# A four-layer graph network on one core: the order of work around layers 1 and 2, with two chunks' slab sums stored later

## The chip, the cores and the metric

The kernel runs on 1 core of one Trainium2 chip. The metric is the device time of one execution in microseconds (us). Engines are named as in the profile: PE (TensorE matmul), PEld (TensorE weight load), DVE (VectorE), ACT (ScalarE), POOL (GpSimd), SP (SyncE, which here issues most DMAs).

## What is computed

A stack of four layers on 3327 nodes with 256 features each, every layer in the form x = x + layer(relu(layernorm(x)), adj). The adjacency matrix is 3327 x 3327, sparse in its values but stored dense.

```
x = x + adj @ (h @ W0.T + b0)                                     # layer 0
sim = tanh(adj * adj) * (adj > 0); keep the 700 largest of a row   # layer 1
x = x + relu(sim @ (tanh(h @ Wp + bp) @ Wg) + bg)
A = adj + I; d = A.sum(1) ** -0.5                                  # layer 2
x = x + relu((d[:, None] * A * d[None, :]) @ (h @ W2.T))
# layer 3: two steps of propagation with (adj + I), rows scaled to sum 1,
# and of top-p attention over all nodes; projections; a last layer norm
```

Layers 0 to 2 are each a product of the whole adjacency matrix with node rows; layer 3 has such products too, and attention.

## The kernel before

**Tiles and products.** The nodes are 26 blocks of 128, taken as two halves of 13; a *pair* p is block p with block p + 13. Each layer multiplies 2 x 2 quadrants of slabs (128 x 128 tiles of the transposed adjacency matrix, loaded by SP) with seven products in place of eight. For that DVE makes four sums of slabs for each chunk (`Feed.adding`, L607 to L610: s1, a difference written over quadrant 21, s2, s4) and four sums of nodes for each stretch of node rows (`combining_nodes`, L396 to L399, into the tile `ts`). In layer 2 the identity is added to diagonal slabs first (L606).

**Layer 0** goes pair by pair, in three chunks of node blocks (`CUTS`). A pair's seven products gather in one `ps_row` tile of two banks; `result` adds them up on DVE (L683 to L688), `finish0` makes the new rows of x (L931 to L937), and the next layer's nodes follow: layer norm (L416, L417, the root on POOL at L125, L433), transposes on PE (`turn`, L445), and a projection (`hidden`, L457, then L504 on DVE and L505 on ACT).

**Layers 1 and 2** go by *doubles* of two pairs (pair 12 alone at the end), in five chunks of 3, 3, 3, 2, 2 node blocks (three chunks for pair 12). `Double.steps` (L744) runs in each chunk through the products in the order 1, 2, 5, 4, 6, 3, 7, one matmul for a node block; a step is one such matmul (two records in the profile), so that in a chunk of three blocks steps 0 to 2 are product 1, 3 to 5 product 2, 6 to 8 product 5, 9 to 11 product 4, 12 to 14 product 6. Products 1, 2, 4, 5 gather in the first of two accumulator tiles, 6, 3, 7 in the second. Both have the tag "row" of the pool `ps_row`, which holds two buffers: a double takes both, and so does its successor. `Double.result` reads the first tile with two ACT copies (L777), and the second with DVE (L779, L781, L782, the last of which completes y1). `weighed` (L789) then multiplies y0 and y1 with the layer's weights, and `finish1` or `finish2` makes the new rows of x.

**What sets the order.** PE's order is written by hand: a layer is a sequence of steps, and `hooks` say after which step of the next double (or pair) an older one's stage is put (its weighing, its turn, its keys). DVE, ACT, POOL and SP are put in order by a scheduler from priorities and due times. `Feed.upto(n)` issues, ahead of chunk n, the loads as far as chunk n + 2 and the sums as far as chunk n + 1, and stores of sums. Slab tiles have three buffers, so a chunk's loads wait until PE has released the chunk three before it.

**Kept sums.** Layer 3 needs the same slab sums as layer 0. They are kept in `s_dram`: those in `KEPT_FIRST` are stored by SP (L637) during layer 0, the others (`KEPT_LATER`) in layer 2; for stored sums of layer 0 POOL adds the identity in layer 3 (L1401).

**Around the change.** At the start of layer 1 (`doubles`, L800 on), pair 11's and pair 12's turn and projection of layer 0's results still come as hooks (30, 40) of the first double; node sums of blocks 9 to 11 are combined ahead of everything and those of block 12 in the last chunk. At the end of layer 2 what remains of the last stages runs after the last product: keys (`add_nodes`, L290: four times a projection into one bank of `ps_acc`, read by ACT at L298 and L302) and the weighing of pair 12. Layer 3 begins with four DVE sums over all node rows (`combining`, L1379 to L1382), the sum of the keys (L1172), their mean on PE (L1168), their centring on DVE (L1179, L1182), and the logits (L1202), among products with slabs (L1462).

Of the kernel before, what the change touches and what calls it, by code (L numbers as in the profile page):

```python
# [11 lines left out]
F32 = mybir.dt.float32  # L12
# [5 lines left out]
ALU = mybir.AluOpType  # L18
AX = mybir.AxisListType
# [5 lines left out]
P = 128  # L25
# [5 lines left out]
H = T // 2  # L31
CUTS = ((0, 5), (5, 9), (9, 13))
# [2 lines left out]
    (p, k)  # L35
    for p in range(2, H)
    for c, (a, b) in enumerate(CUTS)
    if (p + c) % 3
    for k in range(a, b)
}  # L40
PIECE = 6
# [15 lines left out]
def kernel(  # L57
# [22 lines left out]
    nc = tc.nc  # L80
# [86 lines left out]
    def merged(*plans):  # L167
        out = {}
        for p in plans:
            for k, v in p.items():  # L170
                out.setdefault(k, []).extend(v)
        return out
# [109 lines left out]
    def add_nodes(kT, ksum, xT, m, name, bank):  # L282


        n = P
        acc = bank(f"pkq_{name}")
        r, col = (0, m) if m < LOW else (DA, m - LOW)
        i = 0 if m < LOW else 1
        for c in range(NC):
            nc.tensor.matmul(  # L290
                acc[:, :n], kq[:, c, i : i + 2].rearrange("p i e -> p (i e)"), xT[:, c, :n],
                start=(c == 0), stop=(c == NC - 1),
            )
        q = DA - r
        real_n = min(n, N - m * P)
        at = slice(m * P, m * P + n)
        with tc.high_priority():
            nc.scalar.activation(  # L298
                kT[r : r + DA, col * P : col * P + real_n], acc[r : r + DA, :real_n], AF.Copy,
                accum_out=ksum[r : r + DA, m : m + 1],  # L300
            )
            last_key.append(nc.scalar.copy(qT[q : q + DA, at], acc[q : q + DA, :n]))  # L302
        nc.scalar.dma_start(qT[r : r + DA, at], qT[q : q + DA, at])
# [9 lines left out]
    def layers_0_to_2(again):  # L313
# [11 lines left out]
        tag = "b" if again else "a"  # L325
# [75 lines left out]
        def combine_nodes(rhs, a, b):  # L401
            run(combining_nodes(rhs, a, b))
# [60 lines left out]
        class Pair:  # L463
# [60 lines left out]
                with tc.high_priority():  # L524
                    nc.scalar.copy(self.rhs.pair(self.p), acc)

            def keys(self):
                for i in range(2):
                    m = self.p + i * H
                    add_nodes(kT0, ksum0, self.xT[:, :, i * P : (i + 1) * P], m, f"{self.name}_{i}", self.bank)  # L530


        def scaled_nodes(p, rhs, x2):
# [20 lines left out]
        class Feed:  # L554
# [67 lines left out]
            def upto(self, n):  # L622


                self.store(n - 1)
                for k, (ahead, what) in enumerate(((2, self.load), (1, self.add))):
                    while self.done[k] < min(n + ahead + 1, len(self.order)):
                        what(*self.order[self.done[k]])
                        self.done[k] += 1
                    if not k:  # L630
                        self.store(n)
# [58 lines left out]

        WHERE = {2: (48, 64), 4: (20, 34, 50, 64)}

        def products(rhs, feed, finish, pair_after, following, counted, begin):

# [98 lines left out]
        def doubles(layer, rhs, feed, w, finish, todo, at_first, places, pair_after, following=None, counted=None):  # L795

            if not todo:
                for c in CUTS:
                    combine_nodes(rhs, *c)
            n = 0  # L800
            for p in range(0, H, 2):
                prod = Double(layer, p, rhs, feed, w)
                first = not p and todo
                if first:
                    combine_nodes(rhs, CUTS[2][0], H - 1)
                hooks = dict(zip(places[prod.many - 1] if p else at_first, todo))
                if counted:
                    hooks[88] = functools.partial(counted, p, prod.many)
                for c, (a, b) in enumerate(cuts(prod.many)):
                    feed.upto(n)  # L810
                    for k, l in ((a, b - 1), (b - 1, b)) if first and b == H else ((a, b),):
                        if first and l == H:
                            combine_nodes(rhs, k, l)
                        for at in prod.steps(c, k, l):
                            if at in hooks:
                                hooks[at]()
                    n += 1
                    if prod.many == 1 and c and following:
                        combine_nodes(following, *CUTS[c - 1])
                feed.upto(n)  # L820
                left = todo[len(places[prod.many - 1]) :] if p else []
                prod.result()
                pairs = []

                def out(p, t, prod, pairs):
                    acc = prod.weighed(t)
                    with tc.high_priority() if p == H - 1 else nullcontext():
                        x2 = feed.x2.pop(p + t)
                        finish(p + t, x2, acc)
                        pairs.append(pair_after(p + t, x2))  # L830

                todo = [functools.partial(out, p, t, prod, pairs) for t in range(prod.many)]
                if layer == 2:
                    for stage in (Pair.turn, Pair.keys):
                        for t in range(prod.many):
                            todo.append(functools.partial(lambda what, pairs, t: what(pairs[t]), stage, pairs, t))
            if layer == 1:
                return todo
            for what in (*left, todo[0]):
                what()  # L840
            return pairs[0]

        def of_double(p):
# [66 lines left out]
        if not again:  # L910
# [138 lines left out]
            def second_layer(p, x2):  # L1049
# [3 lines left out]

            left = doubles(
                1, rhs1, Feed(1, OF_DOUBLES, from_rows(x1_dram), change=filtered, many=of_double), late_weights["wg"],
                finish1, left, (30, 40), ((20, 32), (10, 16)), second_layer, following=rhs2,
            )
        else:
            def x1_pair(p):
# [54 lines left out]
        left = doubles(  # L1114
            2, rhs2,
            Feed(2, OF_DOUBLES, from_rows(x2_dram), count=count2, keep=() if again else KEPT_LATER, many=of_double), w2s,
            finish2, left, (10,), ((20, 32, 56, 72), (10, 16, 38, 44, 52, 60)), lambda p, x2: Pair(3, p, h3, x2),
            counted=done2,
        )
        return lctx, h3.rows, kT0, ksum0, left  # L1120
# [16 lines left out]
    def layer_3_in(again, tag, big, ep, w3, sm3, h3, kT0, ksum0, left):  # L1137
# [20 lines left out]
        def constants():  # L1158
            for i in range(2):
                nc.scalar.dma_start(u1s[:, :, i, :], u1t[i].rearrange("(c p) e -> p c e", p=P))  # L1160
                nc.scalar.dma_start(u2s[:, :, i, :], u2t[i].rearrange("(c p) e -> p c e", p=P))

        def key_sum(kT, ksum, name):
            total = sm3.tile([P, 1], F32, tag="ktotal", name=f"ktotal_{name}{tag}")

            def by_tensor():
                pk = one_bank(f"pk_mean_{name}{tag}")
                nc.tensor.matmul(pk[:, :1], halves, total, start=True, stop=True)  # L1168
                return pk

            with tc.high_priority():
                nc.vector.tensor_reduce(total, ksum, AX.X, ALU.add)  # L1172
            return by_tensor

        def centre(kT, pk, name):
# [664 lines left out]
        with tc.manual_schedule(engines=PE_ALONE):  # L1840
# [3 lines left out]
            def prepare(step, m, kT):  # L1844
                made[m] = scores(step, m, kT)
                return made[m][2]
# [37 lines left out]
            def propagate_first(n, at):  # L1884

                d, phase = divmod(n, 4)
                x = firsts.setdefault(d, FirstPropagation(d)) if d not in firsts else firsts[d]
                units = len(x.units(phase))
                run(x.steps(phase), {int(k * units // T): v for k, v in at.items()})
                if n != T - 3 and n != T - 1:  # L1890
                    x.keep(phase)

            def whole_run(steps, at):

                return {at: [lambda: next(steps)]}
# [29 lines left out]
            for i in range(EARLY):  # L1925
                if i == 0:
                    left.pool, left.bank = (w3, "eT", 3), one_bank
                    mean0 = []

                    def sum_keys():  # L1930
                        mean0.append(key_sum(kT0, ksum0, "0"))

                    def centre_keys():
                        centre(kT0, mean0[0](), "0")

                    propagate_first(0, dict(zip((15, 18, 19, 22), ([what] for what in (*left.stages, sum_keys, centre_keys)))))
                    with tc.issue_after(last_key[-1].ins):
                        constants()
                    next(sums_of_first)
                elif i == 1:  # L1940
                    propagate_first(1, merged(whole_run(prepare(0, 0, kT0), 3), {12: [lambda: next(sums_of_first)]}))
                    run(find(0, 0, st0))
                    with tc.issue_after(added[-1].ins):
                        kT1, ksum1 = new_keys(f"1{tag}", big)
                else:
                    propagate_first(i, whole_run(prepare(0, i - 1, kT0), 3))
                    finder = find(0, i - 1, st0)
                    if i + 1 < EARLY:
                        run(finder)
# [250 lines left out]
```

## Time and profile before

| | |
|---|---|
| runs | 2493.24, 2492.91, 2490.91 us; median 2492.91 |
| profiled execution | 2493.01 us, of which the span of the profile is 2491.2 us |
| PE busy | 2449.1 us (98%) |
| DVE, ACT, POOL busy | 2079.9, 1074.7, 293.6 us |
| layer 1 begins, layer 2 begins, its products end | 332.7, 632.3, 928.4 us |
| SP's DMA packets | 367.5 MB on its main queue, 156 GB/s in all |

The profile lists groups of instructions by line, engine and operation; `out<-in` are tile names, `x` the count, then busy time, mean of one in ns, and the engine's idle time just before the group with what ended most of it. A row of the timeline is start, length, engine, line, operation, tiles, count, and in brackets the idle time before it and what released it. Times within the span are us from its start. Two records of L755 are one step of a double.

### The profile page before, as it was taken

The page shows a single profiled execution, that of the slowest core. Times are in us where ns is not written, and L with a number is a line of the kernel's source. Part 1 is how long each engine was busy: PE and PEld are TensorE (multiplying, and loading weights), DVE is VectorE, ACT ScalarE, POOL GpSimd, SP SyncE. Part 2 cuts the span into 40 slices and gives each one's busy share as a digit, 9 for nine tenths or more (in the row PEclk, how much of TensorE's full clock was granted, in tenths as well). Part 3 has the DMA queues.
Part 4 walks back from the last instruction along what each step waited for, and adds up shares of the span by engine and source line. Part 5 has one row for each costly group of instructions (what it writes and reads, how often), then busy time and mean ns, then how long its engine had stood idle before and what let it go on. Part 6 is the DMA issues. An engine that isn't in the chain of part 4 may idle for free. (4 is left out here: it accounts for less than half of the span.)

```text
span 2491.2 us, 41120 instructions
## 1 busy us (share of the span) xinstructions
PE 2449.1 (98%) x14483; PEld 2104.5 (84%) x14483; DVE 2079.9 (83%) x5306; ACT 1074.7 (43%) x2074; POOL 293.6 (12%) x466
## 2 busy tenths in 40 slices
PE   9999989999999999999999999999999999999997
PEld 8999978888888897777777777777788888888887
DVE  7877788888876758888788797885899999999994
ACT  3000034343011115556556665654556555655551
POOL 2000010000000000000000100000112322222232
PEclk9999999999999999999999999999999999999999
DMA  6788856565968656423232324324534443444343
GB/s 203 250 274 265 281 178 188 165 186 161 314 216 266 213 157 215 124 66 101 87 107 84 104 67 122 97 72 122 178 94 130 143 122 114 135 140 125 114 140 109
DMA packets 278675, 387.79 MB, mean 156 GB/s; under 512 B 24253, under 2 KB 216250, under 8 KB 278458
## 3 DMA queue, kind: packets, MB, share of 16 engines
q1 hardware_dynamic: 257322, 367.54, 47.7%
q10 hardware_dynamic: 21136, 17.52, 2.1%
q8 instruction: 116, 1.90, 0.3%
q14 instruction: 101, 0.83, 0.1%
HBM read 315.37 MB, written 67.89 MB: 154 GB/s over the span
## 5 line engine op out<-in xcount | busy, mean ns | idle before, releaser
L226 ACT COPY eT_a<-pt_a 128x512 f32<-128x512 f32 (+1 forms) x364 | 196.4, 554 | 377.3 <-PE pt_a L223 374.9
L234 PE MATMUL a<-h3a,eT_a 128*128 128x256 f32 x1352 | 321.6, 381 | 2.2 <-ACT eT_a L226 2.2
L234 PE MATMUL a<-vs,eT_a 128*128 128x256 f32 x1352 | 320.2, 381 | 0.2 <-ACT eT_a L226 0.2
L1289 DVE MAX8 cand_a<-w 128x8 f32<-128x128 f32 x1352 | 284.9, 278 | 3.9
L234 PEld LDWEIGHTS a<-h3a,eT_a 128*128 128x128 f32 x1352 | 246.1, 189 | 48.9 <-issue 10.0
L234 PEld LDWEIGHTS a<-vs,eT_a 128*128 128x128 f32 x1352 | 244.8, 190 | 30.3 <-ACT eT_a L226 0.7
L1285 DVE SCALAR_TENSOR_TENSOR w<-e_a,t_a 128x896 f32<-128x896 f32 x208 | 230.0, 1106 | 3.6
L223 PE MATMUL pt_a<-ident,e_a 128*128 128x128 f32 x1352 | 198.4, 272 | 2.5 <-DVE e_a L1304 2.5
L1227 ACT ACTIVATE e_a<-pl_a 128x1024 f32<-128x1024 f32 x260 | 184.7, 729 | 36.0 <-PE pl_a L1202 35.6
L1276 DVE SCALAR_TENSOR_TENSOR w<-e_a,t_a 128x3328 uint8<-128x3328 f32 x52 | 192.2, 3695 | 4.8 <-DVE t_a L1273 0.5
L223 PEld LDWEIGHTS pt_a<-ident,e_a 128*128 128x128 f32 x1352 | 166.3, 141 | 32.4 <-issue 3.1
L1304 DVE SCALAR_TENSOR_TENSOR e_a<-e_a,all_least 128x3328 f32<-128x3328 f32 x52 | 191.9, 3690 | 1.8
L755 PE MATMUL acc_a<-s_a,tsa 128*128 128x256 f32 (+1 forms) x728 | 170.5, 367 | 11.3 <-DVE s_a L607 10.4
L755 PE MATMUL acc_a<-a_a,tsa 128*128 128x256 f32 (+1 forms) x728 | 173.5, 365 | 0.0
L899 ACT ACTIVATE a_a<-a_a 128x768 f32<-128x768 f32 (+2 forms) x132 | 98.8, 749 | 166.0 <-DVE a_a L897 139.5
L1462 PE MATMUL f0a<-slab3a_0a,tsa 128*128 128x256 f32 (+1 forms) x728 | 161.1, 367 | 0.0
L755 PE MATMUL acc_a<-a_a,rhs 128*128 128x256 f32 (+1 forms) x728 | 158.4, 364 | 2.1 <-ACT y_a L777 2.1
L1260 ACT ACTIVATE junk_a<-e_a,t_a 128x3328 uint8<-128x3328 f32 x52 | 159.8, 3073 | 0.4
L755 PEld LDWEIGHTS acc_a<-s_a,tsa 128*128 128x128 f32 x728 | 132.2, 191 | 28.2 <-DVE s_a L607 10.8
L1265 ACT ACTIVATE junk_a<-e_a,t_a 128x3328 uint8<-128x3328 f32 x50 | 153.3, 3066 | 0.0
L1521 PE MATMUL f1a<-tsa,slab3a_1a 128*128 128x128 f32 x1248 | 148.1, 276 | 0.0
L755 PEld LDWEIGHTS acc_a<-a_a,rhs 128*128 128x128 f32 x728 | 130.0, 190 | 18.5 <-ACT y_a L777 2.6
(281 smaller groups left out, 4339.5 us busy)
## 6 DMA issues: line engine op xcount, KB each, us to landing
a_a<-in_adj_t_dram SPq DMA_DIRECT2D x216, 256.0 KB, 3.5
a_a<-in_adj_t_dram SPq DMA_DIRECT2D x144, 384.0 KB, 4.1
slab3a_0a<-s_dram SPq DMA_DIRECT2D x95, 384.0 KB, 4.0
slab3a_0a<-in_adj_t_dram SPq DMA_DIRECT2D x65, 384.0 KB, 3.9
slab3a_1a<-s_dram SPq DMA_DIRECT2D x60, 384.0 KB, 4.0
a_a<-in_adj_t_dram SPq DMA_DIRECT2D x60, 320.0 KB, 4.4
slab3a_1a<-in_adj_t_dram SPq DMA_DIRECT2D x48, 384.0 KB, 3.9
s_dram<-s_a SPq DMA_DIRECT2D x45, 256.0 KB, 4.9
```

The lines of the kernel that those rows point to most:

```text
L223: nc.tensor.transpose(pt[:, j, :], e[:, k * P : (k + 1) * P], ident)
L226: last_turned.append(nc.scalar.copy(eT[:, : len(blocks), :], pt[:, : len(blocks), :]))
L234: nc.tensor.matmul(acc[:, :width], ready[g][:, j, :], rhs[:, k, :], start=(k == 0), stop=(k == T - 1))
L755: nc.tensor.matmul(self.acc[n], t, slab[:, :, k - cuts(self.many)[c][0], :], start=(k == 0 and n in (1, 5, 6, 7)), stop=(k == H - 1 and n ...
L1227: last_exp.append(nc.scalar.activation(dst, src, AF.Exp, accum_out=parts[:, c : c + 1]))
L1260: nc.scalar.activation(junk_a, e, AF.Relu, scale=-1.0, bias=t, accum_out=short)
L1265: nc.scalar.activation(junk_a, e, AF.Sign, scale=-1.0, bias=t, accum_out=sign)
L1276: nc.vector.scalar_tensor_tensor(junk, e, t, e, ALU.is_lt, ALU.mult, accum_out=got)
L1285: nc.vector.scalar_tensor_tensor(w[:, : (b - a) * P], eg, t, eg, ALU.is_lt, ALU.mult, accum_out=below[:, g : g + 1])
L1289: nc.vector.max(cand[:, 8 * k : 8 * k + 8], w[:, (k - a) * P : (k - a + 1) * P])
L1304: nc.vector.scalar_tensor_tensor(e, e, least, e, ALU.is_ge, ALU.mult, accum_out=st["kept"][:, m : m + 1])
L1462: nc.tensor.matmul(self.acc[:, self.at[n]], right_half(h3, ts, n, k), self.block(phase, at), start=not at, stop=at == len(units) - 1, skip ...
```

## The change

The instructions on PE, DVE and ACT are the same in number; their order changes, and so do eight stores on SP and four additions on POOL.

- `KEPT_FIRST` loses chunks 1 and 2 of pair 12: eight stores of 256 KB, four for each chunk, move from the end of layer 0 to layer 2's last chunks.
- `Feed.upto` in layers 1 and 2: at the first chunk, it is loaded and its sums are issued before the loads of the two chunks after it.
- `doubles`: the node sums of layer 1's first double are made for each of its last two chunks just ahead of it, (9, 11) and (11, 13), instead of (9, 12) ahead of all and (12, 13) inside the last.
- Hooks: layer 0's stages from steps 48, 64 to 54, 68 (and the last of four from 64 to 65); the weighing of a double from 10, 16 to 14, 20, of pair 12's time from 20, 32 to 26, 36; turns and keys in layer 2 from 38, 44, 52, 60 to 40, 46, 54, 62, and from 56, 72 to 56, 70, 84; layer 2's first from 10 to 14.
- The end of layer 2: pair 10's keys come inside pair 12's steps (84), and pair 11's two use the two banks of one `ps_row` tile.
- Layer 3: the fourth of the node sums over all rows (L1382) is issued after the sum of the keys (L1172).

```diff
     for c, (a, b) in enumerate(CUTS)
-    if (p + c) % 3
+    if (p + c) % 3 and (p, c) not in ((H - 1, 1), (H - 1, 2))
     for k in range(a, b)
...
-            def keys(self):
+            def keys(self, banks=None):
                 for i in range(2):
                     m = self.p + i * H
-                    add_nodes(kT0, ksum0, self.xT[:, :, i * P : (i + 1) * P], m, f"{self.name}_{i}", self.bank)
+                    bank = banks[i] if banks else self.bank
+                    add_nodes(kT0, ksum0, self.xT[:, :, i * P : (i + 1) * P], m, f"{self.name}_{i}", bank)
...
                 self.store(n - 1)
+                if not n and self.layer:
+                    for k, what in enumerate((self.load, self.add)):
+                        what(*self.order[0])
+                        self.done[k] = 1
...
-        WHERE = {2: (48, 64), 4: (20, 34, 50, 64)}
+        WHERE = {2: (54, 68), 4: (20, 34, 50, 65)}
...
                 first = not p and todo
-                if first:
-                    combine_nodes(rhs, CUTS[2][0], H - 1)
...
                     feed.upto(n)
-                    for k, l in ((a, b - 1), (b - 1, b)) if first and b == H else ((a, b),):
-                        if first and l == H:
-                            combine_nodes(rhs, k, l)
-                        for at in prod.steps(c, k, l):
-                            if at in hooks:
-                                hooks[at]()
+                    if first and b > CUTS[2][0]:
+                        combine_nodes(rhs, a, b)
+                    for at in prod.steps(c, a, b):
+                        if at in hooks:
+                            hooks[at]()
...
-            for what in (*left, todo[0]):
-                what()
+            held = ps_row.tile([P, 2, 512], F32, tag="row", name=f"keys_{tag}")
+            (last,) = left
+            last([lambda name, i=i: held[:, i, :] for i in range(2)])
+            todo[0]()
...
-                finish1, left, (30, 40), ((20, 32), (10, 16)), second_layer, following=rhs2,
+                finish1, left, (30, 40), ((26, 36), (14, 20)), second_layer, following=rhs2,
...
-            finish2, left, (10,), ((20, 32, 56, 72), (10, 16, 38, 44, 52, 60)), lambda p, x2: Pair(3, p, h3, x2),
+            finish2, left, (14,), ((26, 36, 56, 70, 84), (14, 20, 40, 46, 54, 62)), lambda p, x2: Pair(3, p, h3, x2),
...
             with tc.high_priority():
-                nc.vector.tensor_reduce(total, ksum, AX.X, ALU.add)
+                summed.append(nc.vector.tensor_reduce(total, ksum, AX.X, ALU.add))
...
-                    propagate_first(1, merged(whole_run(prepare(0, 0, kT0), 3), {12: [lambda: next(sums_of_first)]}))
+                    def last_sums():
+                        with tc.issue_after(summed[-1].ins):
+                            next(sums_of_first)
+
+                    propagate_first(1, merged(whole_run(prepare(0, 0, kT0), 3), {12: [last_sums]}))
```

More of the change, by code (lines that the diff above doesn't have):

```diff
@@ L835, in doubles @@
                         for t in range(prod.many):
-                            todo.append(functools.partial(lambda what, pairs, t: what(pairs[t]), stage, pairs, t))
+                            todo.append(functools.partial(lambda what, pairs, t, *banks: what(pairs[t], *banks), stage, pairs, t))
             if layer == 1:
                 return todo
-            for what in (*left, todo[0]):
-                what()
+            held = ps_row.tile([P, 2, 512], F32, tag="row", name=f"keys_{tag}")
+            (last,) = left
+            last([lambda name, i=i: held[:, i, :] for i in range(2)])
+            todo[0]()
             return pairs[0]
@@ L1161, in constants @@
                 nc.scalar.dma_start(u2s[:, :, i, :], u2t[i].rearrange("(c p) e -> p c e", p=P))
+        summed = []
         def key_sum(kT, ksum, name):
```

## The prediction

> **What bounds the kernel now.** I read the busy list first, then the groups with their idle time, then TensorE's timeline gap by gap.
>
> ```profile
> PE 2449.1 (98%) x14483; PEld 2104.5 (84%) x14483; DVE 2079.9 (83%) x5306; ACT 1074.7 (43%) x2074; POOL 293.6 (12%) x466
> ...
> L755 PE MATMUL acc_a<-s_a,tsa 128*128 128x256 f32 (+1 forms) x728 | 170.5, 367 | 11.3 <-DVE s_a L607 10.4
> ```
>
> PE is busy 98% of the span. The change keeps every matmul, so it can win only idle time of PE, 42.1 us in all. One group holds 10.4 us of it. In PE's timeline at the start of layer 1:
>
> ```profile
> 332.74 2.76 PE L755 MATMUL acc_a<-a_a,rhs 128*128 128x256 f32 x12
> 345.89 2.93 PE L755 MATMUL acc_a<-s_a,tsa 128*128 128x256 f32 x6 [10.40 <-DVE s_a L607]
> 348.62 1.79 PE L755 MATMUL acc_a<-a_a,tsa 128*128 128x256 f32 x6
> 350.25 1.46 PE L755 MATMUL acc_a<-s_a,tsa 128*128 128x256 f32 x6
> ```
>
> Products 1 and 2 need raw slabs and run; product 5 waits for the slab sum s1 (L607). The six records after the wait took 2.93 and 1.79 us, against 1.46 later. The windows over this wait show why:
>
> ```profile
> 336.00:338.00 2.00, 0.00 (x0) 0.00 (x0) 2.00 (x5) 0.45 (x1) 0.00 (x0) 1.00 0.00 0
> 338.00:340.00 2.00, 0.00 (x0) 0.00 (x0) 2.00 (x9) 1.61 (x3) 0.01 (x1) 0.76 0.00 0
> 340.00:342.00 2.00, 0.00 (x0) 0.00 (x0) 2.00 (x6) 0.00 (x0) 2.00 (x1) 0.50 0.00 0
> ```
>
> Columns: window, length, busy PE, PEld, DVE, ACT, POOL, then granted clock, DMA share, GB/s. DVE (third) is full, so PE waits for DVE's order, not for data. The clock falls to 0.50 while PE idles; 345.89 to 350.25 is 4.36 us where 2.60 was due, 1.76 us more. A later gap of 2.06 us (before 388.78) shows 1.00.
>
> A steady double of layer 1, on PE:
>
> ```profile
> 431.71 2.75 PE L755 MATMUL acc_a<-a_a,rhs 128*128 128x256 f32 x12
> 434.30 1.46 PE L755 MATMUL acc_a<-s_a,tsa 128*128 128x256 f32 x6
> 435.60 1.03 PE L755 MATMUL acc_a<-a_a,tsa 128*128 128x256 f32 x4
> 436.46 1.41 PE L789 MATMUL out_a<-wgsa,y_a 128*128 128x256 f32 x4
> 438.64 1.13 PE L789 MATMUL out_a<-wgsa,y_a 128*128 128x256 f32 x4 [0.77 <-DVE y_a L782]
> ```
>
> Two records are one step, 0.433 us. After 11 steps PE weighs the previous double (L789); half of that (4 records, 0.87 us) runs, then it waits 0.77 us for L782, the last sum of that result.
>
> **Part by part.** The sum is against the profiled execution, 2493.01 us (span 2491.2); the median of the runs is 2492.91, so either base gives the same forecast.
>
> *Turn in layer 0, 48 to 54.* The gaps before the transposes L445 are 1.24 us (to 252.48) and 0.33 (to 275.73), both for DVE's xn (L433). Six steps of two records (10 records at L661 span 1.11 us, 0.22 a step) are 1.3 us or more. Both go: **+1.5**. The weighing products that follow move too and wait for nothing.
>
> *Start of layer 1.* In the new DVE order s1 of the first chunk stands after two filters of the second, at about 331.1, where it stood at 344.91. I replayed DVE's order with its measured pitches (768 wide .87, 512 wide .60, 256 wide .35, filters no earlier than their slabs' landing now). s1 is done at 332.0, before product 5 is due at 335.5. What is late next is product 6: it opens the second accumulator, which the last pair of layer 0 still holds until L688. DVE comes to that at 340.4, where product 6 is due at 337.9: a wait of 2.5. Then s1 of the second chunk, behind the norm that waits for POOL (1.75 us from 344.9 to 346.75 now), is done at 348.7, due at 347.0: 1.75. The sums of nodes 9 to 11 (done 369.1) meet their use at about 369: nothing. PE starts pair 2 at 378.8 instead of 388.78, and there waits 2.2 in front of product 6 for L782 (386.2). Waits become 2.5+1.75+2.2 = 6.45; they were 10.39+1.76 (clock)+2.06 = 14.2: **+7.8**. Bounds: 4, if slabs land 2 us late twice, or the clock drops once more (1.76); 11, if two of the three waits close.
>
> The clock: by the rows a gap of 2.06 us costs nothing and one of 10.39 does, so 2.5 lies near the harmless end; I take nothing, up to 1.76. The Trainium skill (TensorE: Matmul & The Clock Gate, Part 1, "What's actually happening") says that the clock halves after an idle window of some 3.4 us that runs freely. The fall between 338 and 340 fits it, and by it no remaining gap would cost clock, so its sum is the same as mine.
>
> *Weighing at step 14 instead of 10 (doubles).* This looks like it gives DVE four more steps, 1.73 us, against a gap of 0.77. But steps 12 to 14 are product 6, and it writes the second accumulator tile, whose two buffers the previous double holds until L782 has read products 6, 3 and 7. So PE now stops in front of step 12 for the same L782. A row shows that this wait exists, in the single pair 12, where product 6 comes before the hook:
>
> ```profile
> 612.89 0.46 PE L755 MATMUL acc_a<-s_a,tsa 128*128 128x128 f32 x2 [0.85 <-DVE y_a L782]
> ```
>
> Before, 11 steps and half a weighing (0.87) were done ahead of the wait; after, 12 steps. PE has 0.87−0.43 = 0.43 us less to do there, in each double where L782 is late. Layer 1, pairs 4 to 10: 4×0.43: **−1.7**. Pair 12: the row above stays, 0. First double of layer 2: L782 ends at 637.74, 5.47 after the start at 632.27, with no gap. In the new order three more 768-wide operations (2.6) and three fewer of 384 (1.4) lie in the chain of L778 to L782, so it ends near 639.1, and step 12 is due at 637.47: **−1.7** (bounds 0 and −2.5). Layer 2, pairs 2 to 10: L782 comes 5.5 to 6.6 after the start, step 12 at 5.2; the waits sum to some 4, where now gaps and stretched weighings are 1.9: **−2.1** (0 to −4).
> The results leave at most 1.73 us later, thirteen times; the x tiles' stores follow them, and the next x loads wait for those in SP's queue ahead of slab loads. SP already waits 167 us there for PE's releases between 400 and 640, so that is nothing; uncovered, it would be 1.73 each.
>
> *End of layer 2.* The keys of pair 11 no longer share banks: the gaps 0.28 and 0.73 for qT (L302) go, **+1.1**. Pair 10's keys merely move forward. Then, DVE and PE:
>
> ```profile
> 944.45 1.89 DVE L1381 TENSOR_TENSOR tsa<-h3a,tsa 128x1664 f32<-128x1664 f32 x1
> 946.26 0.17 DVE L1172 TENSOR_REDUCE ktotal_0a<-ksum_0a 128x1 f32<-128x26 f32 x1
> ...
> 946.58 0.35 PE L1168 MATMUL pk_mean_0a<-ktotal_0a,halves 128*128 128x1 f32 x2 [1.35 <-DVE ktotal_0a L1172]
> ```
>
> The key sum stood behind node sums. With the last one after it, L1172 runs 1.8 us sooner and PE's 1.36 goes: **+1.3** (1.0 to 1.36). The moved sum then stands before the centring L1182, which PE's logits need at 949.99; it fills DVE's wait of 0.54 and PE has other products until then.
>
> *Stores.* Eight stores of 256 KB leave SP's queue before layer 1, where DMA is 0.84 busy (320 to 330): help that I price at nothing. They join the queue after 905 and, at 4.9 us each to land with several in flight, end near 925; the first slab of layer 3 is issued at 935.33, and DMA is 0.20 busy from 920 to 940. Nothing, unless that slab slips over 2 us. Four POOL additions fewer (1 us each) lie beside PE's work.
>
> Sum: 1.5+7.8−1.7−1.7−2.1+1.1+1.3 = **6.2**. 2493.01−6.2 = **2486.8**.
>
> **Rivals.** *A, weighing gaps vanish:* product 6 doesn't bind, because L782 moves up as DVE gets free. For it: DVE idles at times in layer 2. Against: 612.89, and L778 to L782 keep their neighbours in DVE's order. Then 5.2 of gaps go (four of about 0.75, 0.85, 0.76, 0.56) instead of −5.5, and two boundary waits of about 2 close: 6.2+10.7+2 = 19, 2474.
> *B, the boundary wait moves on:* DVE is busy 59.5 of the 70 us from 320 to 390, and sums done early push filters and node sums back; waits at chunks 2 to 5 eat half. Gain there 4, sum 2.4: 2490.6.
> *C, slower:* L782 falls behind one more DVE operation (0.87 us) in each of the 13 doubles, since finishing the result also moves; every such delay now stops PE in front of product 6 with nothing else to do. 13×0.87 = 11.3 against 6.2: 2498. It decides from 0.5 us a double; over 0.2% from 0.86.
> *D, slabs late in layer 3* from the moved stores: each us past 2 costs one; it would have to be 8 to turn the sign, so I give it no case.
>
> **Numbers.** This kernel's runs tell 0.2%, 5 us, from no change. Forecast 0.55 (its own range 2482 to 2492, 0.40 of it faster by over 5 us), A 0.13, B 0.20 (0.04 faster), C 0.12. Faster 0.57, same 0.31, slower 0.12. The range 2476 to 2494 takes in the forecast, B and the near edges of A and C.
>
> **What would show it.** Right: the 10.40 at L607 gone, with a wait of 2 to 3 us for L688 in front of product 6 and no clock under 0.9 there; in each double of layers 1 and 2 a wait of 0.3 to 1.5 us in front of step 12 named L782, and none at L789; no gap at L302 or L1172. Wrong: no waits at step 12 (A); waits for s_a in chunks 2 to 5 of the first double above 6 us together (B); waits at step 12 near 2 us (C); a gap at L1462 near 940 (D).

## The result, and the profile after

The changed kernel took 2492.49 us (median of 14 runs, 2488.01 to 2496.23), the kernel before 2491.67 (14 runs, 2489.23 to 2493.24): a ratio of 1.0006, 95% interval 0.9998 to 1.0014. That is no change. The range of the prediction holds it; its likeliest time, 2486.8, is 5.7 us too low, and "faster" was its likeliest case.

The profiled execution of the changed kernel took 2488.01 us, the lowest of its 14; that of before, 2493.01, was near the top of its own. Set side by side, these two alone would have said 5 us faster. So the rows below say *where* waits stand; how much they are worth is left to the runs.

The same lines have higher numbers in the changed kernel: the matmul of a double is L760 (was L755), the slab sums L608 to L611 (L607 to L610), the copies L782 (L777), the sums of a result L783 to L787 (L778 to L782, the last of which completes it), the weighing L794 (L789), layer 0's last sum L693 (L688), and the filter, the DVE operation that layer 1 applies to each raw slab, L901 (L897). In the runs below the shift is 0 to 5.

The busy list and the group that held the 10.4 us:

```profile
PE 2446.3 (98%) x14483; PEld 2104.3 (85%) x14483; DVE 2077.0 (84%) x5306; ACT 1073.5 (43%) x2074; POOL 280.5 (11%) x462
...
L760 PE MATMUL acc_a<-s_a,tsa 128*128 128x256 f32 (+1 forms) x728 | 169.7, 366 | 17.9 <-DVE y_a L787 16.4
```

The idle time ahead of this group grew from 11.3 to 17.9 us, and its main releaser is now L787. The wait for s1 is all but gone; a wait for the result of the double before is there instead. At the start of layer 1, PE's timeline:

```profile
329.92 2.76 PE L760 MATMUL acc_a<-a_a,rhs 128*128 128x256 f32 x12
332.51 1.46 PE L760 MATMUL acc_a<-s_a,tsa 128*128 128x256 f32 x6
333.81 1.46 PE L760 MATMUL acc_a<-a_a,tsa 128*128 128x256 f32 x6
335.10 1.46 PE L760 MATMUL acc_a<-s_a,tsa 128*128 128x256 f32 x6
...
343.26 1.56 PE L760 MATMUL acc_a<-s_a,tsa 128*128 128x256 f32 x6 [1.52 <-DVE s_a L608]
...
354.88 1.56 PE L760 MATMUL acc_a<-a_a,rhs 128*128 128x256 f32 x6 [1.42 <-ACT rhs L505]
```

Product 5 (332.51) follows product 2 at once. What stays in this double are 1.52 us for the second chunk's s1 and 1.42 for a projection. A double of layer 1, on PE and then on DVE:

```profile
419.53 2.75 PE L760 MATMUL acc_a<-a_a,rhs 128*128 128x256 f32 x12
422.12 1.46 PE L760 MATMUL acc_a<-s_a,tsa 128*128 128x256 f32 x6
423.42 1.46 PE L760 MATMUL acc_a<-a_a,tsa 128*128 128x256 f32 x6
426.28 1.53 PE L760 MATMUL acc_a<-s_a,tsa 128*128 128x256 f32 x6 [1.41 <-DVE y_a L787]
427.65 1.89 PE L794 MATMUL out_a<-wgsa,y_a 128*128 128x256 f32 x8
```

```profile
419.51 0.42 DVE L783 TENSOR_TENSOR y_a<-y_a 128x256 f32<-128x256 f32 x1
419.84 1.82 DVE L901 SCALAR_TENSOR_TENSOR a_a<-a_a 128x768 f32<-128x768 f32 x2
421.58 0.42 DVE L784 TENSOR_TENSOR y_a<-y_a,acc_a 128x256 f32<-128x256 f32 x1
421.91 0.95 DVE L901 SCALAR_TENSOR_TENSOR a_a<-a_a 128x768 f32<-128x768 f32 x1
422.78 0.69 DVE L785 TENSOR_TENSOR y_a<-y_a,y_a 128x512 f32<-128x512 f32 x1
423.38 0.95 DVE L608 TENSOR_TENSOR s_a<-a_a,a_a 128x768 f32<-128x768 f32 x1
424.25 0.42 DVE L786 TENSOR_TENSOR y_a<-y_a,acc_a 128x256 f32<-128x256 f32 x1
424.58 0.96 DVE L901 SCALAR_TENSOR_TENSOR a_a<-a_a 128x768 f32<-128x768 f32 x1
425.45 0.69 DVE L787 TENSOR_TENSOR y_a<-y_a,acc_a 128x512 f32<-128x512 f32 x1
```

Product 6 (426.28) starts when L787 has released its accumulator, after 12 steps; the weighing behind it waits for nothing. DVE puts five 768-wide operations among the five small ones of the result, so that these take 6.6 us from first to last.

### The profile page after: what moved, and what is told of

Its sections match the earlier page's. It is cut to its first block, busy times and chain, and to the rows that moved or that the text cites. A ratio compares the mean times of both kernels' runs of the same rounds, so it can differ in the third digit from the quotient of the medians.

```text
span 2486.0 us, 41120 instructions
## 1 busy us (share of the span) xinstructions
PE 2446.3 (98%) x14483; PEld 2104.3 (85%) x14483; DVE 2077.0 (84%) x5306; ACT 1073.5 (43%) x2074; POOL 280.5 (11%) x462
## 5 line engine op out<-in xcount | busy, mean ns | idle before, releaser
L760 PE MATMUL acc_a<-s_a,tsa 128*128 128x256 f32 (+1 forms) x728 | 169.7, 366 | 17.9 <-DVE y_a L787 16.4
L760 PE MATMUL acc_a<-a_a,tsa 128*128 128x256 f32 (+1 forms) x728 | 169.6, 365 | 0.0
L760 PEld LDWEIGHTS acc_a<-s_a,tsa 128*128 128x128 f32 x728 | 129.7, 190 | 37.9 <-issue 16.6
L760 PE MATMUL acc_a<-a_a,rhs 128*128 128x256 f32 (+1 forms) x728 | 158.5, 364 | 1.4 <-ACT rhs L505 1.4
L1527 PEld LDWEIGHTS f1a<-tsa,slab3a_1a 128*128 128x128 f32 x1248 | 144.0, 192 | 1.8
```

Of the source, the lines that this page charges most:

```text
L760: nc.tensor.matmul(self.acc[n], t, slab[:, :, k - cuts(self.many)[c][0], :], start=(k == 0 and n in (1, 5, 6, 7)), stop=(k == H - 1 and n ...
L1527: nc.tensor.matmul(self.accs[bank][:, c * P : (c + 1) * P], self.block(phase, at)[:, 0, :], right_half(self.h, self.ts, n, k), start=start ...
```

## The experiments

Theory 1: the start of layer 1 gains what was forecast, and the later weighing gives it back, because product 6 stands in front of it and waits for the accumulator. Theory 2: the waits at product 6 are an accident of the execution, or come from L787 wherever the weighing stands. All ratios are to the kernel before, run on the same chip, with 95% intervals.

**The changed kernel again** (`e1_after_again`, nothing edited).

> The changed kernel, nothing edited, for a second profile. Theory 1 (the start of layer 1 gains, the later weighing gives it back): waits of 1.3 to 2.8 us in front of product 6 in every double again, 12 to 14 us together in layers 1 and 2, and the time within 0.2% of before. Theory 2 (the waits at product 6 of the first profile are an accident of one execution): they differ by more than half between the two profiles. What differs between executions should be the start of layer 1, where the wait of 1.52 in the first profile may become 3 to 6.

1.0008 (0.9999 to 1.0017), 2494.57 us, 11 runs from 2491.13 to 2499.63. The waits in front of product 6 are there again, 15.6 us in all where the first profile has 16.4: theory 1. They are less even than was expected, 0.49 to 2.50 us here and 0.62 to 2.73 there. The waits at the start are 1.60, 1.52 and 1.42; the 1.52 did not grow. Of the 6.8 us by which this execution's span exceeds the first profile's, 2.8 are there by product 6 of layer 1's second double (384.69 against 381.90): layer 1 begins 1.0 us later, and the 1.60 us, a wait for layer 0's last sum (L693), is absent in the first profile. Another 3.1 come between 632.79 and 818.98, where the clock drops twice; see the last section.

**Only the weighing, both ways.** Put back in the changed kernel (`e2_hooks_back`), and moved alone in the kernel before (`e4_before_hooks`):

```diff
-    finish1, left, (30, 40), ((26, 36), (14, 20)), second_layer, following=rhs2,
+    finish1, left, (30, 40), ((20, 32), (10, 16)), second_layer, following=rhs2,
-    finish2, left, (14,), ((26, 36, 56, 70, 84), (14, 20, 40, 46, 54, 62)), lambda p, x2: Pair(3, p, h3, x2),
+    finish2, left, (10,), ((20, 32, 56, 70, 84), (10, 16, 40, 46, 54, 62)), lambda p, x2: Pair(3, p, h3, x2),
```

```diff
-    finish1, left, (30, 40), ((20, 32), (10, 16)), second_layer, following=rhs2,
+    finish1, left, (30, 40), ((26, 36), (14, 20)), second_layer, following=rhs2,
-    finish2, left, (10,), ((20, 32, 56, 72), (10, 16, 38, 44, 52, 60)), lambda p, x2: Pair(3, p, h3, x2),
+    finish2, left, (14,), ((26, 36, 56, 72), (14, 20, 38, 44, 52, 60)), lambda p, x2: Pair(3, p, h3, x2),
```

> The changed kernel with the weighing put back to steps 10, 16 (20, 32 for pair 12; 10 at the start of layer 2). Theory 1: product 6 no longer waits, L794 shows gaps of 0.5 to 0.8 as in the kernel before, and the time falls by about 9 us (6.2+2.7+5.0 of waits less 4.9 of gaps), so 7 to 9 under before. Theory 2 (the waits follow L787's lateness and come wherever the weighing stands): within 2 us of the changed kernel.

> The kernel before with only the weighing moved to steps 14, 20 (26, 36 for pair 12; 14 at the start of layer 2). Theory 1: slower than before by 7 to 10 us, with waits of 1.3 to 2.8 us in front of product 6 in each double. Theory 2: the same as before within 2 us.

e2: 0.9967 (0.9955 to 0.9979), 2485.08 us. e4: 1.0031 (1.002 to 1.0043), 2500.8 against 2492.98 us. The weighing alone costs 7.8 us, and undoing it in the changed kernel brings 7.4 us against its first runs and 9.5 against the repeat on the same chip. Theory 2 falls. In e4 the same wait stands in a kernel that has nothing else of the change, though smaller than expected: 0.35 to 1.76 us a double, and none in the first double of layer 2, where DVE's work between L778 and L782 is as before (5.36 us).

```profile
433.58 1.46 PE L755 MATMUL acc_a<-a_a,tsa 128*128 128x256 f32 x6
436.17 1.53 PE L755 MATMUL acc_a<-s_a,tsa 128*128 128x256 f32 x6 [1.13 <-DVE y_a L782]
437.54 1.89 PE L789 MATMUL out_a<-wgsa,y_a 128*128 128x256 f32 x8
```

**The last place in front of product 6** (`e3_hook_11`).

```diff
-    finish1, left, (30, 40), ((26, 36), (14, 20)), second_layer, following=rhs2,
+    finish1, left, (30, 40), ((19, 31), (11, 17)), second_layer, following=rhs2,
-    finish2, left, (14,), ((26, 36, 56, 70, 84), (14, 20, 40, 46, 54, 62)), lambda p, x2: Pair(3, p, h3, x2),
+    finish2, left, (11,), ((19, 31, 56, 70, 84), (11, 17, 40, 46, 54, 62)), lambda p, x2: Pair(3, p, h3, x2),
```

> The changed kernel with the weighing at steps 11, 17 (19, 31 for pair 12; 11 at the start of layer 2): the last place in front of product 6. Theory 1: PE does 12 steps and half a weighing before it needs L787, 0.43 us a double more than at step 10: 10 to 13 us less than the changed kernel, the fastest of the four. Theory 2: the same as the changed kernel.

0.9953 (0.994 to 0.9967), 2481.02 us: 12 us under before and 4 under e2; one step of 0.43 us for each of ten doubles would be 4.3. The mechanism, by PE's timeline of e3:

```profile
424.91 1.46 PE L760 MATMUL acc_a<-a_a,tsa 128*128 128x256 f32 x6
426.20 1.03 PE L794 MATMUL out_a<-wgsa,y_a 128*128 128x256 f32 x4
427.74 1.13 PE L794 MATMUL out_a<-wgsa,y_a 128*128 128x256 f32 x4 [0.51 <-DVE y_a L787]
428.70 1.46 PE L760 MATMUL acc_a<-s_a,tsa 128*128 128x256 f32 x6
```

All of product 4 and half of the weighing run while DVE finishes; 0.51 us of wait is left.

**Only the start of layers 1 and 2** (`f1_start_only`), and that **with the stores** (`f2_start_stores`).

```diff
+                if not n and self.layer:
+                    for k, what in enumerate((self.load, self.add)):
+                        what(*self.order[0])
+                        self.done[k] = 1
...
-                if first:
-                    combine_nodes(rhs, CUTS[2][0], H - 1)
...
+                    if first and b > CUTS[2][0]:
+                        combine_nodes(rhs, a, b)
```

```diff
-    if (p + c) % 3
+    if (p + c) % 3 and (p, c) not in ((H - 1, 1), (H - 1, 2))
```

> The kernel before with only the start of layers 1 and 2 changed (first chunk loaded and summed first, node sums before chunks 4 and 5). Theory 1: the wait of 10.4 for s1 and the half clock after it go, what stays is 1.5 to 2.5 in front of product 6 (last pair of layer 0) and about 1.5 for the second chunk's s1, and 1.4 for a projection: 7 to 10 us under before. Rival B of the prediction: the waits move on into chunks 2 to 5, 4 us or less under before.

> The same, and the eight stores moved from the end of layer 0 to the end of layer 2. If the stores held back slabs at the start of layer 1, the first filters start 1 to 3 us earlier and the time falls by 1 to 2 us against the run without it; if they cost nothing there and nothing at the end, the same within 1 us; if they hold back layer 3's first slabs, a gap at the products of layer 3 (L1462 here) appears near 930 and the time rises by it.

f1: 0.9971 (0.9959 to 0.9982), 2484.79 against 2492.88 us. Rival B falls: waits for L692, s1 and L505 are 1.61, 1.52 and 1.36, and that double has no others. f2: 0.9975 (0.9963 to 0.9987), 2485.84 us, from 2481.05 to 2490.65, which can't be told apart from f1; there is no gap at layer 3's first slabs.

**Only layer 0's steps, the keys and the key sum** (`f3_ends_only`: the changed kernel with the weighing, the start and the stores as before).

> The kernel before with only layer 0's steps (54, 68), the keys at the end of layer 2 and the key sum in layer 3 changed. Prediction's terms: 1.5 + 1.1 + 1.3 = 3.9 us under before. By the profile of the changed kernel: 1.5 + 0.15 + 1.36 = 3.0, with a gap of 0.85 between the two keys of pair 11.

1.0005 (0.9996 to 1.0013), 2493.37 us against 2492.88: a gain of 3 us is excluded, and so is any above 1 us.

**Two of the waits that were left** (`g1_turn_keys`, on top of e3).

```diff
-    finish1, left, (30, 40), ((19, 31), (11, 17)), second_layer, following=rhs2,
+    finish1, left, (30, 47), ((19, 31), (11, 17)), second_layer, following=rhs2,
...
-            last([lambda name, i=i: held[:, i, :] for i in range(2)])
+            last([bank, lambda name: held[:, 0, :]])
```

> The changed kernel with the weighing at steps 11, 17 and two more edits: pair 12's projection at the start of layer 1 at step 47 instead of 40, behind product 2 of the third chunk, which then need not wait for it (gap of 1.41 at rhs, L505, gone); and pair 11's two keys in a bank of each of two pools (gap of 0.85 at qT, L302, gone). If both gaps only go: 1 to 3 us under the kernel with steps 11, 17 alone, so 12 to 15 under before. If the projection comes too late, waits for s_a or the sums of nodes in chunk 4 take its place and the time is the same.

0.9949 (0.9936 to 0.9962), 2478.99 us. Both gaps are gone and no wait took their place. What that is worth is not resolved: 13.9 us under before here, 12.0 for e3 on another chip, with intervals that overlap. At the end of layer 2, the changed kernel and then g1:

```profile
926.00 0.61 PE L290 MATMUL keys_a<-xT_a,kq 128*128 128x128 f32 x4
927.45 0.71 PE L290 MATMUL keys_a<-xT_a,kq 128*128 128x128 f32 x4 [0.85 <-ACT qT L302]
928.00 1.89 PE L794 MATMUL out_a<-w2sa,y_a 128*128 128x256 f32 x8
```

```profile
917.59 0.61 PE L290 MATMUL pkq_a<-xT_a,kq 128*128 128x128 f32 x4
918.04 0.61 PE L290 MATMUL keys_a<-xT_a,kq 128*128 128x128 f32 x4
918.49 2.09 PE L794 MATMUL out_a<-w2sa,y_a 128*128 128x256 f32 x8
```

**What the rest of the change is worth on this base.** Start, steps 11, 17 and 47 in the kernel before (`h1_start_weigh`, on top of f1); with the key sum first (`h2_key_sum`); h1 with the stores (`h3_stores`); and g1 again, which has all of it (`h4_all_again`).

```diff
-    finish1, left, (30, 40), ((20, 32), (10, 16)), second_layer, following=rhs2,
+    finish1, left, (30, 47), ((19, 31), (11, 17)), second_layer, following=rhs2,
-    finish2, left, (10,), ((20, 32, 56, 72), (10, 16, 38, 44, 52, 60)), lambda p, x2: Pair(3, p, h3, x2),
+    finish2, left, (11,), ((19, 31, 56, 72), (11, 17, 38, 44, 52, 60)), lambda p, x2: Pair(3, p, h3, x2),
```

> The kernel before with the start of layers 1 and 2 changed, the weighing at steps 11, 17 (19, 31 for pair 12) and pair 12's projection at step 47: nothing of layer 0's steps, the stores, the keys or the key sum. Start 8.1 (measured) + weighing 4 + projection 1.4: about 13 us under before, and 1 to 2 us above the kernel that has all of these and the rest of the change, if the rest is worth the key sum's 1.2 and the keys' 1.0; equal to it if the rest is worth nothing.

> The same, and the key sum issued ahead of the fourth node sum in layer 3. If its 1.36 of wait is a gain: 1.2 to 1.4 us under the kernel without it, with no gap at pk_mean and the logits 1.6 us sooner after layer 3's first product. If the wait moves on to a later step of layer 3: the same within 0.5.

> The first of these four, and the eight stores moved to layer 2. If they matter at the start of layer 1: layer 1 begins, or its wait for the last pair of layer 0 ends, up to 1.3 us sooner, and the time is lower by that. If not, the same within 1 us, with no gap at layer 3's first slabs.

> The changed kernel with the weighing at 11, 17, the projection at 47 and the keys in two pools, again: 13 to 15 us under before, and the lowest of the four by 1 to 2 us if the key sum, the keys and layer 0's steps are worth 1.2, 1.0 and nothing.

0.9946, 0.9947, 0.9945 and 0.9951, each with an interval of about 0.0013 to either side: medians of 2479.82, 2478.92, 2478.76 and 2479.86 against 2492.38 us. The four can't be told apart, and `h4_all_again`, expected to be the lowest by 1 to 2 us, is not. The start, the place of the weighing and the projection at step 47, which h1 has alone, make the whole 12.6 us; the rest is below what five runs with a spread of 4 to 9 us resolve (about 3 us).

## Why the prediction was right or wrong

The parts, each run alone, add up: start −8.1, weighing +7.8, layer 0's steps, keys and key sum together +0.5, stores nothing that shows. That is +0.2, and the whole was measured at +0.8 (14 runs each) and +1.6 (the repeat), intervals −0.5 to +3.5 and −0.2 to +4.2. So the prediction named the two large terms and their signs, and missed the balance by its sizes. It forecast 6.2 us less and 0.8 more were measured. Of these 7.0 us, 4.4 lie in the three small terms (layer 0's steps, keys and key sum: 3.9 forecast, −0.5 in f3) and 2.3 in the weighing. That the range holds the result is owed to its width, which was made to take in other cases: the forecast's own range ended at 2492, and the outcome "same" had been given a chance of 0.31.

- **Start of layer 1, +7.8: right**, 8.1. Inside it the terms shift, and that they add up is in part luck. The wait for layer 0's last sum was put at 2.5 us; it is 0 in the first profile and 1.60 in the second. s1 was computed for about 331 and came at 325.58 in the first profile: DVE reached the first filter at 320.31 (before: 324.05) and no longer waited for slabs behind it (before: 0.91 and 0.73 us). The second chunk's s1 was put at 1.75: 1.52. The second double's wait was put at 2.2: 1.71 and 1.64. The wait of 1.42 for the projection (L505) was not seen at all; with it the waits of the second profile sum to 6.18 us, where 6.45 was forecast.
- **Weighing, −1.7−1.7−2.1 = −5.5: the mechanism was right, the size too small**, −7.8 by the medians. In layer 1, 0.43 us more a double would make 1.20 of the gap of 0.77; in the changed kernel the gaps are 1.41, 1.74, 1.73 and 1.31. These rows overstate the loss, since before the change a part of the wait lay inside the weighing (its first four records take 1.41 us at 436.46, and 1.03 in e3 at 426.20). The first double of layer 2 was put at 1.7 and is 2.73 and 2.50: in the first profile its sums on DVE take 6.56 us instead of 5.36, as reckoned, but they begin 1.36 us after the double's start, where they began 0.11 after it. Layer 2's later ones were put at some 4 in all, and are 5.0. From the end of the first double's result in layer 1 to that of the last result in layer 2, the later weighing costs 5.3 us in the first profile (381.75 to 927.79, against 384.87 to 925.58 in e2), 8.1 in e1 (384.54 to 933.35) and 7.4 in e4 (391.91 to 935.05, against 394.43 to 930.22 before). The clock drops in this stretch in e1 alone; the prediction took that as nothing. What makes e4 dearer than 5.5 stays open.
- **Layer 0, +1.5: wrong.** The gaps of 1.24 and 0.33 belong to the one execution that was profiled. Layer 1 began at 332.74 us there, but at 330.00 to 330.53 in the six other profiles with the same old steps, and at 329.92 to 330.94 in the seven with the new ones.
- **Keys, +1.1: wrong**, 0.15 by the rows. The gaps of 0.28 and 0.72 became one of 0.85: the second projection still waits until the first is read, although it has a bank of its own in the tile. With a tile from another pool it does not (g1).
- **Key sum, +1.3: right as a row, open as time.** PE's wait for it is gone, and from layer 3's first product to the logits it is 14.60 us in each profile with the change and 16.19 or 16.20 in each without. Some 0.5 of that is lost again between the logits and a later wait of PE for e_a (L1304 before): 745.4 to 745.9 us without the change, 746.0 to 747.0 with it. Neither f3 nor h2 shows the remainder in the time.
- **Stores, 0: right** as far as the runs resolve. The wait for layer 0's last sum has a mean of 2.2 us in three profiles without the move (1.61, 2.90, 2.09) and 0.9 in eight with it; whether that is worth a microsecond stays open.
- Of the rivals, A (weighing gaps vanish) and D (late slabs) are excluded by the rows, and B by f1. C named the right mechanism, PE stopped in front of product 6 with nothing else to do, but its cause, one more operation ahead of L787, did not happen in layer 1: the five operations among the result's are the same in both kernels. In the first double of layer 2 the result does come later on DVE, as said above.

## What to carry to other kernels

Before a consumer is moved later to give its producer time, look at what the engine would then run first: if that needs a buffer which the same producer releases, the wait is not shortened but brought forward. Of the three places tried here, the last one in front of the step that needs the buffer was the best. And a gap of about a microsecond in one profile is a term of a sum only if a second execution shows it too.

## What the runs showed of the hardware

The granted clock can halve after waits of PE of about 2 us, which the prediction put near the harmless end, and it does not do so in each execution. The first double of layer 2 in the second profile of the changed kernel (e1), after a wait of 2.50 us that ended at 632.79; then in the first, after 2.73 us that ended at 630.40 (columns as in the prediction):

```profile
632.00:634.00 2.00, 1.21 (x5) 1.13 (x6) 2.00 (x4) 0.00 (x0) 0.00 (x0) 0.93 1.02 332
634.00:636.00 2.00, 2.00 (x6) 1.53 (x6) 2.00 (x4) 0.00 (x0) 0.00 (x0) 0.50 0.45 155
636.00:638.00 2.00, 2.00 (x8) 1.63 (x7) 0.68 (x2) 0.00 (x0) 0.00 (x0) 0.72 0.00 0
```

```profile
630.00:632.00 2.00, 1.60 (x8) 1.45 (x9) 2.00 (x4) 0.00 (x0) 0.00 (x0) 1.00 1.08 344
632.00:634.00 2.00, 2.00 (x11) 1.77 (x10) 2.00 (x4) 0.00 (x0) 0.00 (x0) 1.00 0.13 47
```

The shorter wait cost clock and the longer one did not. e1 has such a drop after a wait of 1.92 us too (0.78 from 768 to 772, 0.79 to 776).

The record of the granted clock in the traces shows where the difference lies. In each of the 14 profiles the clock changes only at whole multiples of 3.413 us from its first rise, which comes 4.5 to 7.6 us after the start. In e1 it falls at 633.71 and 770.24, 40 × 3.413 us apart, and each time for one such stretch. A drop goes with how long PE idles within one stretch. Over the first 2400 us of all profiles, each stretch with 2.00 us or more of idle PE was followed by half clock in the next one (the shortest are 2.00 in h2, 2.02 in e2, 2.26 in e3, 2.49 in e1, 2.53 in h1). Around 1.95 us it goes either way: 1.92 (e1) was followed by a drop, 1.94 (before) and 1.98 (the changed kernel) were not. None below 1.9 was. The wait of 2.50 us lay within one stretch (630.29 to 633.71); that of 2.73 was divided at 629.65 into 1.98 and 0.75. In e3 two waits of 1.49 and 0.77 us fell into one stretch, and the clock dropped. Idle time is not all of it: near the end of e4 a stretch with 1.74 us was followed by a drop too (at 2459.70).

In e1 the two drops can cost 3.4 us (3.41 us at half clock, twice). That is at most half of the 6.8 us by which the two executions of the same kernel differ; the start of layer 1 has 2.8 of it. Whether such drops make the spread of the times is not shown: f1 stays within 2483.9 to 2485.6 over six runs and has no wait above 1.61 us in layers 1 and 2, but f2, with none above 1.52 in its profile, goes from 2481.1 to 2490.7.

The Trainium skill (TensorE: Matmul & The Clock Gate, Part 1, "What's actually happening") puts the fall after an idle window of some 3.4 us that runs freely. That stretches of this length run freely, so that the fall depends on where in time a wait lies, agrees with these traces; that a whole stretch has to be idle does not, since 1.92 us was enough here.

Not tried: to keep the five operations of a double's result next to each other on DVE, which might bring L787 forward.
